# Later steps for softmax sums that go by DRAM, an earlier root in an output loop, and a depthwise stage cut differently

## The chip, the cores and the metric

The kernel runs on one core of one Trainium2 chip. The metric is the device time in microseconds (us), the median of several runs. The profile comes from one further execution. Its engines are PE (matrix products), DVE (vector), ACT (activation functions and copies), POOL and SP, which here only issues transfers (DMA). Each engine works through its own instructions in program order, and waits for others by semaphores.

## The reference, cut to what matters

Four layers follow each other on x of shape (4, 256, 64, 64); every layer is added to its input, and takes the input after a group norm. Two pieces of it are what the change touches most: the softmax of layer 0's attention, and the depthwise and pointwise products of layer 2.

```python
# layer 0, after a 3x3 convolution, group norm and relu (xs)
f = jnp.einsum('bnc,bcm->bnm', theta_x, phi_x)
attn = jax.nn.softmax(f, axis=-1)
y = jnp.einsum('bnm,bmc->bnc', attn, g_x)
...
w_y = group_norm(conv1x1(y, w_w, w_b), gn2_w, gn2_b)
return w_y * 0.1 + xs
# layer 1, the end of it: linear attention, projection, norm over channels
out = jnp.einsum('oc,bchw->bohw', w_out, out) + b_out[None, :, None, None]
out = rmsnorm(out, g_out)
# layer 2: kernels made from the image; dk is (B, C, 3, 3), pk is (B, O, C)
dw = lax.conv_general_dilated(xr, kr, (STRIDE, STRIDE), [(PAD, PAD), (PAD, PAD)], feature_group_count=B * C, dimension_numbers=('NCHW', 'OIHW', 'NCHW'))
out = jnp.einsum('bchw,boc->bohw', dw, pk) + bias[None, :, None, None]
# layer 3: four experts mixed into one 1x1 convolution
```

## The kernel before, in words

An image has 256 channels, two halves of 128 partitions, and 4096 pixels. [...] a matrix product of 512 columns is two passes of PE.

**Images overlap.** While PE works through the attention of image b (`attend`), the rest of image b-1's layers (`tail`) and the convolution of image b+1 (`convolve`, `convolve_second` for image 1) are woven into it. Two Python generators do this: `run` takes one step of a `Chain` of layers and one of the attention in turn, and the order in which they call instructions is the order on every engine. For image 3, the last, there is no attention left to hide its tail; instead, 16 output products of image 2 (`held`, filled in by `w.fill` and ended by `w.settle`) are put between its parts.

**The attention** goes through 8 blocks of 512 queries with 16 steps each. A step computes two tiles of logits (`pf`, line 986), ACT takes exp into `pr` (line 987), PE accumulates `py` (line 1096), DVE adds `pr` to `tot` (line 124, the helper `tt`). At the end of a block, `ended_by_dram` divides `py` by the softmax sums. The sums lie across partitions in 128 x 512 values, so they are turned through DRAM: store to `sum_d` (line 1017), reload transposed into `inv` (line 1020), reduce and reciprocal on DVE (lines 1025 to 1027), store to `rec_d` (line 1028), broadcast back (line 1032), multiply (`yq<-yq,inv`), project (`ps_wy`, line 1040), copy into `wt` (line 1041), statistics and store (lines 1003, 1004). Each bare `yield` in it is one step of the next block's attention, so the yields set the place of each instruction in the order of its engine, and of each transfer in SP's queue. The other transfers on that queue are the convolution's filters (line 478, three buffers, loaded one product ahead), image copies (line 661), and loads of layers. The last block of an image takes another way (`ended`).

**The convolution** makes tiles `v` on DVE from rows of the image (`ra`, `rt`), which PE multiplies by the filters `u` into `ps_conv` (line 584 in image 1's, line 512 in the others').

**The output loop of `linear_attention`** goes through 8 blocks of 512 pixels. `outputs` makes the product `ps_o` (line 1339) and four sums of squares on ACT (line 1341). `root` clamps on DVE (line 1346) and takes the power -1/2 on POOL (line 217). `scaled` multiplies by it: for the last image (`alone`) three quarters on ACT (line 1355) and one on DVE (line 1357). `added` transposes on PE (`ps_zt`, line 1368), adds on DVE and takes statistics (line 1370).

**The depthwise stage of the last image, `shared_out`.** There are 8 parts of 1024 pixels: part 2c+h is pixel block c of channel half h. A part is either made on DVE, 8 taps on top of a centre that ACT makes (`taps`, `centre`), or on PE by products with diagonal matrices (`taps_by_products`, line 1557, two halves of 9 products, copied out by ACT on line 1560). Before the change, DVE makes parts 0, 2, 4, 6 and 7, and PE parts 1, 3 and 5. `point` multiplies the two parts of a pixel block by the pointwise kernel `pk` (`ps_pw`, line 1512), which DVE mixes from eight slices (`mix_kernel`); `pointwise_added` adds to the image on DVE (line 1528) and sums squares on ACT (line 1530). All orders in `shared_out` are written out by hand: `diagonal(n)` issues n of PE's products, `go(i, n)` n taps of DVE.

Of the kernel before, what the change touches and what calls it, by code (L numbers as in the profile page):

```python
# [13 lines left out]
P = 128  # L14
NH = 2
HW = 64
# [77 lines left out]
def conv_preact_fast(ctx: ExitStack, tc: tile.TileContext, guard, x, wc, wtpg, ww, wqkv, wout, w1cat, wd2,  # L94
# [864 lines left out]
    def attend(b):  # L959
# [48 lines left out]
        def ended_by_dram(q, py, tot):  # L1008


            at = b * NQ + q
            inv = wk.tile([P, 512], F32, tag="inv", name="inv")
            nc.vector.scalar_tensor_tensor(inv, tot[:, 0:512], 1.0, tot[:, 512:CH], ALU.mult, ALU.add,
                                           accum_out=guard[:, 0, at:at + 1])
            yt = wk.tile([P, 512], F32, tag="yq", name="yq")
            nc.scalar.copy(yt, py)
            nc.sync.dma_start(out=sum_d[at], in_=inv)
            yield
            yield
            nc.sync.dma_start(out=inv.rearrange("r (p k) -> r p k", k=4), in_=sum_d[at].rearrange("p (r k) -> r p k", k=4))  # L1020
            yield
            yield
            yield
            r = sp.tile([P, 4], F32, name="r_inv", bufs=1)
            nc.vector.tensor_reduce(r, inv.rearrange("r (p k) -> r k p", k=4), AX.X, ALU.add)
            nc.vector.reciprocal(r, r)
            nc.vector.tensor_reduce(guard[:, 1, at:at + 1], r, AX.X, ALU.add)
            nc.sync.dma_start(out=rec_d[at].rearrange("(r k) -> r k", k=4), in_=r)
            xc = residual_block(q) if b == B - 1 else None
            yield  # L1030
            yield
            nc.sync.dma_start(out=inv, in_=rec_d[at].partition_broadcast(P))
            yield
            yield
            tt(yt, yt, inv, ALU.mult)
            yield
            wt = k4("wt").rearrange("p (h n) -> p h n", h=NH)
            for h in range(NH):
                ps = bank("ps_wy")
                nc.tensor.matmul(ps, ww_s[:, bass.ts(h, P)], yt, start=True, stop=True)  # L1040
                nc.scalar.copy(wt[:, h, :], ps)
            if b == B - 1:
                for h in range(NH):
                    residual_stats(q, h, xc)
            yield
            projected(q, wt, xc)
# [166 lines left out]
    def linear_attention(w, b, big, qT, k4, st, sh, sums):  # L1213
# [119 lines left out]
        def outputs(c):  # L1333
            zr = sp.tile([P, 4], F32, name="zr", bufs=3)
            banks = []
            for s in range(2):
                ps = bank("ps_o").rearrange("p (j o) -> p j o", j=2)
                for j in range(2):
                    nc.tensor.matmul(ps[:, j, :], qT[:, bass.ts(4 * c + 2 * s + j, P)], w2, start=True, stop=True)  # L1339
                for j in range(2):  # L1340
                    nc.scalar.activation(junk()[:, 0:NH * P], ps[:, j, :], AF.Square, accum_out=zr[:, 2 * s + j:2 * s + j + 1])  # L1341
                banks.append(ps)
            return zr, banks
# [5 lines left out]
        def scaled(zr, banks):  # L1349
            z = k4("z").rearrange("p (j o) -> p j o", j=4)  # L1350
            if alone:
                for j in range(4):
                    src = banks[j // 2][:, j % 2, :]
                    if j < 3:
                        nc.scalar.activation(z[:, j, :], src, AF.Copy, scale=zr[:, j:j + 1])
                    else:
                        nc.vector.tensor_scalar(z[:, j, :], src, zr[:, j:j + 1], None, ALU.mult)
                return z
            for s in range(2):
                tt(z[:, bass.ts(s, 2), :], banks[s], zr[:, bass.ts(s, 2)].unsqueeze(2).to_broadcast([P, 2, NH * P]), ALU.mult)  # L1360
            return z

        def added(c, z, halves=range(NH)):
            cols = bass.ts(c, 512)
            for h in halves:
                pt = bank("ps_zt")
                for j in range(4):
                    nc.tensor.transpose(pt[:, bass.ts(j, P)], z[:, j, bass.ts(h, P)], ident)
                stt(big[:, h, cols], pt, gains[:, 1, h:h + 1], big[:, h, cols], ALU.mult, ALU.add)
                nc.vector.bn_stats(st[:, h, c, :], big[:, h, cols])  # L1370

        if alone:

            this, last = outputs(0), None
            root(this[0])
            for c in range(NC):
                after = outputs(c + 1) if c + 1 < NC else None
                z = scaled(*this)
                for h in range(NH):
                    if last is not None:  # L1380
                        added(c - 1, last, (h,))
                    if h == 0 and after is not None:
                        root(after[0])
                this, last = after, z
                w.settle()
                if c in (2, 4):
                    w.fill(1)
                yield 1
            added(NC - 1, last)
            w.fill(2)  # L1390
            return st
# [20 lines left out]
    def generated(w, b, big, k4, st, sh, diag):  # L1412
# [117 lines left out]
                    nc.scalar.activation(junk(), big[:, oh, cols], AF.Square, bias=pivot[:, oh:oh + 1],  # L1530
                                         accum_out=sums[:, 1, oh, c:c + 1])

        def taps(i):

            c, h = PARTS[i]
            dst = dw[i].rearrange("p (y x) -> p y x", x=HW)
            for ty, tx in TAPS:
                dx = tx - 1
                x0, x1 = max(0, -dx), min(HW, HW - dx)
                k = h * 9 + 3 * ty + tx  # L1540
                stt(dst[:, :, x0:x1], xp[:, h, c * rows + ty:c * rows + ty + rows, x0 + dx:x1 + dx], dk[:, k:k + 1],
                    dst[:, :, x0:x1], ALU.mult, ALU.add)
                yield 0.62

        def taps_by_products(parts):

            for i in parts:
                c, h = PARTS[i]
                dw[i] = k4("dw")
                for s in range(2):  # L1550
                    ps = bank("ps_dw")
                    dst = ps.rearrange("p (y x) -> p y x", x=HW)
                    for n, (ty, tx) in enumerate([(1, 1)] + TAPS):
                        dx = tx - 1
                        x0, x1 = max(0, -dx), min(HW, HW - dx)
                        y0 = (2 * c + s) * RB + ty
                        nc.tensor.matmul(dst[:, :, x0:x1], diag[:, 3 * ty + tx, :], xp[:, h, y0:y0 + RB, x0 + dx:x1 + dx],  # L1557
                                         start=(n == 0), stop=(n == 8))
                        if n == 8:
                            nc.scalar.copy(dw[i][:, bass.ts(s, 512)], ps)  # L1560
                        yield

# [30 lines left out]
        def shared_out():  # L1593

            slices = [load_wp2(j) for j in range(R // 2)]
            yield from w.pending()
            products = taps_by_products([2 * c + 1 for c in range(N // CH - 1)])
            dw[0] = centre(0)
            for k in range(9):
                nc.scalar.activation(diag[:, k, :], ident, AF.Copy, scale=dk[:, 9 + k:10 + k])  # L1600
            on_vector = {i: taps(i) for i in (0, 2, 4, 6, 7)}

            def go(i, n):
                for _ in range(n):
                    next(on_vector[i])

            def diagonal(n):
                for _ in range(n):
                    next(products)

            def point(c):
                d = [dw[2 * c + h] for h in range(NH)]
                return [(2 * c + s, pointwise_products(s, d)) for s in range(2)]

            dw[2] = centre(2)
            diagonal(24)
            go(0, 8)
            w.settle()
            mix_kernel(slices, range(0, R // 2))
            go(2, 3)  # L1620
            mix_kernel(slices, range(R // 2, R))
            go(2, 5)
            dw[4] = centre(4)
            res = point(0)
            diagonal(12)
            pointwise_added(*res[0])
            go(4, 1)
            pointwise_added(*res[1])
            go(4, 7)
            dw[6], dw[7] = centre(6), centre(7)  # L1630
            res = point(1)
            diagonal(18)
            go(6, 1)
            pointwise_added(*res[0])
            go(6, 2)
            pointwise_added(*res[1])
            go(6, 5)
            go(7, 8)
            res = point(2)
            pointwise_added(*res[0])  # L1640
            res = res[1:] + point(3)
            for r in res:
                pointwise_added(*r)

        if diag is None:
            yield from in_order(range(len(PARTS)))
# [752 lines left out]
```

## Time and profile before

| what | us |
|---|---|
| median of 3 runs (3075.39 to 3075.71) | 3075.55 |
| the profiled execution | 3076.46 |
| its span, from first to last instruction | 3073.7 |
| PE busy | 2980.7 (97%) |
| DVE busy | 2071.8 (67%) |
| ACT busy | 1160.1 (38%) |
| image 0's attention with image 1's convolution | about 200 to 714 |
| last image alone | 2807 to the end |

The span is that of one execution, on the profiler's clock from its first instruction. In the views of the profile a group of instructions is named by its source line, engine, operation, and the tiles that it writes and reads (`v<-ra`). A wait names who ended it; in timelines it stands in square brackets with its length. "SPq" and other names with a q are an engine's sequencer, which waits and issues transfers. A transfer's landing is later than its issue.

### The profile page before, as it was taken

Reading aid. Unit: us, or ns where it says so; the run is one execution under the profiler, and the core shown is the slowest. Engines: PE = TensorE matmul, PEld = TensorE weight load, DVE = VectorE, ACT = ScalarE, POOL = GpSimd, SP = SyncE. Lnnn points to the kernel's source line nnn. Section 1 sums busy time; section 2 is a strip of 40 time slices with the busy share of each in tenths; the row PEclk is TensorE's granted clock in tenths of the full one; section 3 lists DMA queues with packets and bytes.
Section 4 is the critical chain, followed back from the end, with each engine's and each line's share of the span. In section 5 each row is a group of like instructions: output and inputs, shape, how many; then the busy total and the mean of one; then the engine's idle time right before and its main releaser. Section 6 shows DMA issues by size and latency. Waiting matters only on the chain.

```text
span 3073.7 us, 24553 instructions
## 1 busy us (share of the span) xinstructions
PE 2980.7 (97%) x8550; PEld 1475.7 (48%) x8550; DVE 2071.8 (67%) x2836; ACT 1160.1 (38%) x2127; POOL 131.8 (4%) x178
## 2 busy tenths in 40 slices
PE   6899999999999999999999999999999999999998
PEld 3454455445554444444566444444446544444643
DVE  8747667852646995777536797678563669866485
ACT  2334233353555332323364532222336453334621
POOL 0100000000010000000011000000000100000100
PEclk9999999999999999999999999999999999999999
DMA  5235433352212233533410333433440232433021
GB/s 220 79 100 128 70 48 50 42 60 79 69 11 35 38 86 65 110 53 61 126 7 11 52 21 86 137 52 41 103 83 18 18 48 38 31 93 99 8 69 66
DMA packets 532387, 200.55 MB, mean 65 GB/s; under 512 B 470688, under 2 KB 480672, under 8 KB 528032
## 3 DMA queue, kind: packets, MB, share of 16 engines
q1 hardware_dynamic: 528224, 182.12, 29.1%
q0 software_dynamic: 4032, 16.78, 3.0%
q8 instruction: 70, 1.15, 0.2%
q14 instruction: 61, 0.50, 0.1%
HBM read 130.13 MB, written 85.52 MB: 70 GB/s over the span
## 4 chain that ended last, share of the span: by engine, by line
PE 70%; DVE 8%; issue 1%; ACT 1%; POOL 0%; DMA 0%; DVEq 0%; POOLq 0%; ACTq 0%
PE pf L986 21%; PE py L1096 20%; PE ps_qkv L1253 5%; PE ps_conv L512 4%; PE ps_pw L1512 4%; PE ps_ex L1712 3%; PE ps_tp L926 3%; PE ps_o L1339 2%; PE ps_g L931 1%; DVE big L127 1%; PE ps_wy L1040 1%; DVE tot L124 1%; PE ps_ctx L1284 1%; PE ps_ss L1244 1%; PE ps_dw L1557 1%
## 5 line engine op out<-in xcount | busy, mean ns | idle before, releaser
L987 ACT ACTIVATE pr<-pf 128x512 f32<-128x512 f32 x1024 | 602.9, 596 | 1117.4 <-PE pf L986 1070.8
L986 PE MATMUL pf<-tpg 128*128 128x512 f32 x2048 | 969.7, 596 | 0.0
L1096 PE MATMUL py<-pr,tpg 128*128 128x512 f32 x2048 | 963.9, 593 | 2.5 <-ACT pr L987 2.3
L124 DVE TENSOR_TENSOR tot<-tot,pr 128x1024 f32<-128x1024 f32 x448 | 546.2, 1219 | 154.4 <-ACT pr L987 153.2
L1096 PEld LDWEIGHTS py<-pr,tpg 128*128 128x128 f32 x2048 | 389.5, 190 | 496.3 <-issue 477.5
L986 PEld LDWEIGHTS pf<-tpg 128*128 128x128 f32 x2048 | 382.5, 190 | 434.1 <-issue 416.3
L127 DVE SCALAR_TENSOR_TENSOR dw<-xp,dk,dw 128x1008 f32<-128x1008 f32 x208 | 263.0, 1268 | 9.8 <-ACT dw L1504 6.9
L512 PE MATMUL ps_conv<-v,u 128*128 128x512 f32 x384 | 170.9, 593 | 3.6 <-DVE v L124 3.6
L1253 PE MATMUL ps_qkv<-wqkv_s,xg 128*128 128x384 f32 x384 | 129.9, 487 | 0.0
L926 PE MATMUL ps_tp<-big,wtpg_s 128*128 128x512 f32 x256 | 117.4, 602 | 3.0 <-ACT big L684 3.0
L124 DVE TENSOR_TENSOR tpg<-ps_g,bg_s 128x512 f32<-128x512 f32 x32 | 22.1, 692 | 145.0 <-PE ps_g L931 145.0
L512 PEld LDWEIGHTS ps_conv<-v,u 128*128 128x128 f32 x384 | 72.8, 190 | 96.1 <-issue 88.5
L217 POOL TENSOR_TENSOR rstd<-rstd,half 128x2 f32<-128x2 f32 x24 | 17.5, 729 | 2334.4 <-DVE rstd L365 2218.0
L1512 PE MATMUL ps_pw<-dw,pk 128*128 128x512 f32 x224 | 101.3, 592 | 0.0
L1253 PEld LDWEIGHTS ps_qkv<-wqkv_s,xg 128*128 128x128 f32 x384 | 72.2, 190 | 53.6 <-issue 9.6
L1272 DVE TENSOR_REDUCE qs<-qk 128x16 f32<-128x512 f32 x24 | 16.5, 686 | 118.5 <-ACT qk L1266 118.5
L927 ACT ACTIVATE tpg<-ps_tp,btp_s 128x512 f32<-128x512 f32 x64 | 43.8, 686 | 119.0 <-PE ps_tp L926 119.0
L584 PE MATMUL ps_conv<-v,u 128*128 128x256 f32 x288 | 68.4, 392 | 10.0 <-DVE v L124 10.0
L926 PEld LDWEIGHTS ps_tp<-big,wtpg_s 128*128 128x128 f32 x256 | 47.6, 193 | 54.8 <-issue 50.3
L1341 ACT ACTIVATE junk<-ps_o 128x256 f32<-128x256 f32 x128 | 49.1, 384 | 63.5 <-PE ps_o L1339 59.1
L1266 ACT ACTIVATE qk<-ps_qkv,rinv 128x256 f32<-128x256 f32 x96 | 45.6, 475 | 72.1 <-PE ps_qkv L1253 58.7
L124 DVE TENSOR_TENSOR v<-ra 128x1024 f32<-128x1024 f32 x58 | 69.5, 1220 | 0.4
(379 smaller groups left out, 3070.5 us busy)
## 6 DMA issues: line engine op xcount, KB each, us to landing
xp<-in_x_dram SPq DMA_DIRECT2D x16, 1024.0 KB, 7.8
wy_d<-wt SPq DMA_DIRECT2D x32, 512.0 KB, 3.0
wy<-wy_d SPq DMA_DIRECT2D x32, 512.0 KB, 4.1
out_dram<-res SPq DMA_DIRECT2D x64, 256.0 KB, 2.1
xs_d<-big POOLq DMA_DIRECT2D x24, 512.0 KB, 11.9
u<-filters SPq DMA_DIRECT2D x48, 256.0 KB, 2.9
xs<-xs_d SPq DMA_DIRECT2D x24, 512.0 KB, 5.0
u<-rows_d SPq DMA_DIRECT2D x36, 256.0 KB, 3.2
```

The lines of the kernel that those rows point to most:

```text
L124: nc.vector.tensor_tensor(o, a, b, op)
L127: nc.vector.scalar_tensor_tensor(o, a, s, b, op0, op1)
L512: nc.tensor.matmul(ps[oh], u(oh, h), v[:, bass.ts(h, 512)], start=(h == 0), stop=(h == NH - 1))
L584: nc.tensor.matmul(ps[:, bass.ts(oh, IY * IX)], u[i][:, h, bass.ts(oh, P)], v[:, i, bass.ts(h, IY * IX)], start=(h == 0), stop=(h == NH - 1))
L926: nc.tensor.matmul(ps, wtpg_s[:, h, k, :], big[:, h, cols], start=(h == 0), stop=(h == NH - 1))
L986: nc.tensor.matmul(pf, phi[:, bass.ts(2 * m + s, P)], theta[:, bass.ts(q, 512)], start=True, stop=True)
L987: nc.scalar.activation(pr[:, bass.ts(s, 512)], pf, AF.Exp)
L1096: nc.tensor.matmul(py, g[:, bass.ts(2 * m + s, P)], probs[i][:, bass.ts(s, 512)], start=(m == 0 and s == 0), stop=(m == NM - 1 and s == 1))
L1253: nc.tensor.matmul(ps[:, 0:3 * HID], xg[:, h, bass.ts(j, P)], wqkv_s[:, h, :], start=(h == 0), stop=(h == NH - 1))
L1339: nc.tensor.matmul(ps[:, j, :], qT[:, bass.ts(4 * c + 2 * s + j, P)], w2, start=True, stop=True)
L1512: nc.tensor.matmul(ps, pk[:, h * NH * P + oh * P:h * NH * P + (oh + 1) * P], dw[h][:, bass.ts(s, 512)], start=(h == 0), stop=(h == NH - 1))
L1712: nc.tensor.matmul(ps, wm[h][:, bass.ts(oh, P)], big[:, h, bass.ts(c, 512)], start=(h == 0), stop=(h == NH - 1))
```

## The change

It has three parts.

In `ended_by_dram`, the reload of the sums is issued one step earlier, and everything from the reduce on comes later: the reduce by two steps, the broadcast by two, the multiplication, the projection and the store by three.

In the last image's output loop, the root of the next block stands ahead of this block's scaling, where it stood between the two channel halves of the block before.

In the depthwise stage, PE leaves two taps of part 1 to DVE (six taps and the centre are 7 products per half, not 9), and the counts of products between the other steps change with it: 27, 5 and 18 where there were 24, 12 and 18. DVE makes part 7 in two halves of 8 rows, and the pointwise products of the last pixel block are issued as they become possible, between additions and taps.

```diff
             nc.sync.dma_start(out=sum_d[at], in_=inv)
             yield
-            yield
             nc.sync.dma_start(out=inv.rearrange("r (p k) -> r p k", k=4), in_=sum_d[at].rearrange("p (r k) -> r p k", k=4))
-            yield
-            yield
-            yield
+            for _ in range(6):
+                yield
             r = sp.tile([P, 4], F32, name="r_inv", bufs=1)
...
             nc.sync.dma_start(out=inv, in_=rec_d[at].partition_broadcast(P))
-            yield
-            yield
+            for _ in range(3):
+                yield
             tt(yt, yt, inv, ALU.mult)
...
                 after = outputs(c + 1) if c + 1 < NC else None
+                if after is not None:
+                    root(after[0])
                 z = scaled(*this)
-                for h in range(NH):
-                    if last is not None:
-                        added(c - 1, last, (h,))
-                    if h == 0 and after is not None:
-                        root(after[0])
+                if last is not None:
+                    added(c - 1, last)
...
-        def taps(i):
+        def taps(i, some=TAPS, over=slice(0, CH // HW)):
...
-            for i in parts:
+            for i, some in parts:
...
-            products = taps_by_products([2 * c + 1 for c in range(N // CH - 1)])
+            products = taps_by_products([(1, TAPS[:6]), (3, TAPS), (5, TAPS)])
...
-            on_vector = {i: taps(i) for i in (0, 2, 4, 6, 7)}
+            on_vector = {i: taps(i) for i in (0, 2, 4, 6)}
+            on_vector[1] = taps(1, TAPS[6:])
...
-            diagonal(24)
+            diagonal(27)
             go(0, 8)
             w.settle()
             mix_kernel(slices, range(0, R // 2))
             go(2, 3)
             mix_kernel(slices, range(R // 2, R))
+            go(1, 2)
             go(2, 5)
             dw[4] = centre(4)
             res = point(0)
-            diagonal(12)
+            diagonal(5)
...
             go(6, 5)
-            go(7, 8)
+
+            ends = [taps(7, TAPS, slice(s * RB, (s + 1) * RB)) for s in range(2)]
+            for _ in ends[0]:
+                pass
             res = point(2)
+            banks = [[bank("ps_pw") for _ in range(NH)] for _ in range(2)]
+
+            def half(s, h):
+                for oh in range(NH):
+                    nc.tensor.matmul(banks[s][oh], pk[:, h * NH * P + oh * P:h * NH * P + (oh + 1) * P],
+                                     dw[6 + h][:, bass.ts(s, 512)], start=(h == 0), stop=(h == NH - 1))
+
+            half(0, 0)
+            half(0, 1)
+            half(1, 0)
             pointwise_added(*res[0])
-            res = res[1:] + point(3)
-            for r in res:
-                pointwise_added(*r)
+            for _ in ends[1]:
+                pass
+            half(1, 1)
+            pointwise_added(*res[1])
+            for s in range(2):
+                pointwise_added(6 + s, banks[s])
```

## The prediction

> **What bounds the kernel now.** I read the page first, then the chain of waits of TensorE (PE) and of VectorE (DVE), then timelines of the three places that the diff touches.
>
> The page, part 1:
>
> ```profile
> PE 2980.7 (97%) x8550; PEld 1475.7 (48%) x8550; DVE 2071.8 (67%) x2836; ACT 1160.1 (38%) x2127; POOL 131.8 (4%) x178
> ```
>
> PE is busy for 2980.7 of 3073.7 us. So an edit is worth the PE idle time that it removes, plus PE work that it removes where PE is the limit. All idle time together is 93 us.
>
> The waits of PE, and those of DVE (total us, times, longest):
>
> ```profile
> PE ps_conv L584 <- DVE v L124: 10.0, 3, 6.7
> ...
> DVE r_inv L1025 <- DMA inv<-sum_d: 39.6, 6, 11.3
> ...
> DVE yq L124 <- DMA inv<-rec_d: 14.9, 5, 5.2
> ```
>
> All eleven DVE stalls on the softmax sums lie in image 0's attention (240 to 700 us); in images 1 to 3 the reduce starts 0.1 to 30 us after its data have landed. Of 54.5 us of DVE stall only three gaps, 10.0 us, reach PE. The longest, in the timelines of DVE, SP's queue and PE, and in the table by windows (PE, PEld, DVE, ACT, POOL busy, then clock):
>
> ```profile
> 326.01 1.05 DVE L1025 TENSOR_REDUCE r_inv<-inv 128x4 f32<-128x512 f32 x1 [11.30 <-DMA inv<-sum_d]
> ...
> 299.76 0.33 SPq L1017 DMA_DIRECT2D sum_d<-inv  x1
> 300.14 0.93 SPq L478 DMA_DIRECT2D u<-filters  x2
> 301.11 1.13 SPq L661 DMA_DIRECT2D xs_d<-in_x_dram  x2
> 302.34 0.54 SPq L1020 DMA_DIRECT2D inv<-sum_d  x1
> 302.92 29.33 SPq L478 DMA_DIRECT2D u<-filters  x2
> ...
> 328.12 6.69 PE L584 MATMUL ps_conv<-v,u 128*128 128x256 f32 x16 [6.72 <-DVE v L124]
> ...
> 320.00:340.00 20.00, 13.28 (x33) 8.06 (x32) 10.02 (x13) 2.71 (x6) 0.00 (x0) 0.74 0.59 58
> ```
>
> The reload of the sums was issued behind 4 MB of image copy and landed at 325.98; DVE stood at the reduce with the convolution's `v` behind it, and PE ran dry for 6.72 us. Then the 16 matmuls took 6.69 us where the other groups of 16 on this line take 3.6: 3.1 us more at half clock. With what surrounds the two shorter gaps (1.98 us at 486, 1.30 at 602; 2.26 and 1.57 by the spacing of matmuls) the stalls cost 9.9 + 2.3 + 1.6 = **13.8 us** of PE time.
>
> The last image's output loop, DVE and POOL:
>
> ```profile
> 2902.35 0.48 DVE L1357 TENSOR_SCALAR ra<-ps_o,zr 128x256 f32<-128x256 f32 x1 [1.11 <-ACT ra L1355]
> 2902.75 0.74 DVE L127 SCALAR_TENSOR_TENSOR tpg<-ps_zt,gains,tpg 128x512 f32<-128x512 f32 x1
> 2903.53 0.69 DVE L1370 BATCH_NORM_STATS2 st<-tpg 128x6 f32<-128x512 f32 x1
> 2904.14 0.15 DVE L1346 TENSOR_SCALAR zr<-zr 128x4 f32<-128x4 f32 x1
> ...
> 2904.46 1.01 POOL L217 TENSOR_TENSOR zr<-zr,half 128x4 f32<-128x4 f32 x1 [3.45 <-DVE zr L1346]
> 2908.92 1.01 POOL L217 TENSOR_TENSOR zr<-zr,half 128x4 f32<-128x4 f32 x1 [3.45 <-DVE zr L1346]
> ```
>
> One turn is 4.46 us and it is a circle: root on POOL (1.01), three scalings on ACT (1.1), DVE's fourth (0.4), its addition and statistics (1.4), the next root's clamp, 0.3 to POOL. No engine is full.
>
> The depthwise stage, PE and DVE, and the mean of a 512-column DVE operation:
>
> ```profile
> 2970.03 7.13 PE L1512 MATMUL ps_pw<-ra,pk 128*128 128x512 f32 x16 [0.65 <-DVE pk L127]
> ...
> 2992.30 1.27 DVE L127 SCALAR_TENSOR_TENSOR dw<-xp,dk,dw 128x1008 f32<-128x1008 f32 x1 [3.26 <-ACT dw L1504]
> ...
> 3004.84 10.43 DVE L127 SCALAR_TENSOR_TENSOR rt<-xp,dk,rt 128x1008 f32<-128x1008 f32 x8
> ...
> L127 DVE SCALAR_TENSOR_TENSOR pk<-wp,pb,pk 128x512 f32<-128x512 f32 x8 | 6.0, 750 | 0.2
> ```
>
> PE has no gap but 0.65 us from 2949 to 3023; its end comes after the last tap of DVE (3015.2) by 16 matmuls, and the last square on ACT ends at 3024.9.
>
> [...] The reload moves 16384 packets of 16 B and lands 11.2 us after its issue on a quiet queue; the store of the same 256 KB lands in 2.0. [...] the trace shows the 16 B packets only after the copy's 64 KB packets (from 315 us).
>
> **Part A, sums by DRAM.** The reload is issued one step earlier (step 0 of the next block, not 1), the reduce is at step 6 instead of 4, the broadcast at 8 instead of 6, the multiplication at 11 instead of 8, the ps_wy matmuls at 12 and the store at 13, of 16 steps: nothing is added. In block 1 the reload now stands ahead of the filters and the copy on SP's queue: sum_d lands at 301.85, so issue 301.9, landing 11.2 us later at 313, and the reduce is due at about 320. In blocks 2 to 5 the reload keeps its place behind filter loads, and the reduce comes two steps later; a step is 4.1 to 4.7 us (blocks of 65 to 75 us), 8.2 to 9.4 us against stalls of 6.7, 4.8, 7.1 and 9.0. The broadcast gets three steps for two: 4 us against stalls of 2.1 to 5.2. So 13.8 us go, less about 1 for rests: **-12.8** (bounds -8 and -13.8).
>
> What is queued behind: in block 1 the two filter loads and the copy [...] land at about 317 and 329; the first product needs its filters at 320.8, the second (335) needs those behind the copy at 330. Slack 4 and 5 us. The reciprocal store, later on SP, lets filter loads pass it.
>
> Images 1 and 2 pay. At the end of their tail and at the convolution's start the statistics of `wt` (two, 1.2 us) and the multiplication (0.6) move nearer to a DVE chain on which PE waits. At 952 us 0.8 us of idle DVE time covers them, 0.4 is left; at 1246 0.3 (1.2 later, 0.9 of PE work earlier). At 1427 the multiplication leaves the chain (-0.6), but the four ps_wy passes (1.72 us) no longer fill PE's time before the gap; afterwards they fill gaps of 0.51 and 0.65, net about +0.3. Sum 1.0 per image, **+2** (0 to +5 [...]).
>
> **Part B, next root first.** The clamp needs only ACT's four squares, which precede the scalings in ACT's order. Then the circle is open and DVE is the limit: 0.06 + 0.4 + 2 x (0.78 + 0.61) = 3.24 us a turn by start distances, ACT 2.04 + 1.1 = 3.1, PE 2.6. Followed from turn 1: turns 2 to 7 begin at 2901.1, 2904.3, 2909.2, 2912.4, 2916.9 and 2920.1 (two `res` operations of 0.65 and waits of 1.0 and 0.6 for ACT in it); the last statistics end at 2926.1 instead of 2930.6. PE's `ps_ex` pieces at the end need 3.4 us from 2921.5 and stay hidden. If PE gets its bank late in turn 4, it is 0.8 less: **-3.7** (-2.5 to -4.8).
>
> **Part C, depthwise.** Four taps less on PE: 8 passes of 0.425, -3.4. DVE gets two taps of 1.305, +2.6, and its eight last taps as sixteen of half width. That size isn't in the trace: the nearest row (512 columns, 0.750 and a gap of 0.04) gives 0.78 at 504, half the 1008 gives 0.65; I take 0.78, so +2.1. ACT's squares come earlier because part 3 ends after 32 products, not 36: part 6's centre is ready at 2988.3, not 2992.2, and DVE's stall of 3.26 goes. DVE begins part 6 at 2991.6, ends the first half of part 7 at 3010.5, two additions at 3011.7, the second half at 3018.0, the last six additions at 3021.7; the squares on ACT, 0.85 each from 3018.8, end at 3023.9: **-1** (-3.2 with 0.65; +1 if PE's half(1,1) or a copy delays DVE).
>
> **Sum** -12.8 + 2 - 3.7 - 1 = **-15.5**. The profiled execution took 3076.46 (2.8 outside its span), 0.9 above the median; against the median 3075.55 this gives **3060**. A measurement of this kernel can hardly tell less than 0.2%, 6.2 us, from no change.
>
> **Rivals.** (1) The stalls move, not vanish: DVE is busy for 14 to 20 of 20 us in image 0, so it may be DVE's work itself that is late; then A gives 0 to -5 and the time is 3067 to 3073. For it: at 590 to 610 DVE is busy 19.7 of 20. Against: those three gaps all follow a stall. (2) SP's order, slower: [...] the reciprocal store waits for a later reduce, and filter loads behind either come after their product. They land about 3 us after issue and products lie 10 to 14 us apart; it decides once the queue holds a load more than 7 us longer. Ten products in image 0 and in the two other convolutions, each 2 us late, are +20 against -15.5: 3080. Against: SP now waits up to 42.8 us at this store and no PE wait names a filter. (3) C turns into a loss with B small: 3064.
>
> **How the numbers follow.** Forecast (3053 to 3067, case 3 within) 0.75; rival 1 0.17; rival 2 0.05; other 0.03. Of rival 1 about half is within 0.2% (above 3069.4). Faster 0.86, same 0.09, slower 0.05. Range 3053 to 3070: both ends of A and B, and half of rival 1.
>
> **What would show it.** DVE's waits on inv<-sum_d and inv<-rec_d below 5 us in all; no 6.7 us gap and full clock at 320 to 340; POOL roots 3.2 to 3.6 us apart; DVE taps of about 0.78 us; the gap before part 6 gone. Wrong, if PE waits name u<-filters, or gaps before ps_conv stay.

## The result, and the profile after

The changed kernel takes 3058.91 us (median, 3058.19 to 3059.73) against 3075.63 for the kernel before: a ratio of 0.9945, 95% interval 0.9929 to 0.9961, 16.7 us or 0.55% faster. The forecast was 3060, 15.5 faster.

Where the time went is read from places that both programs pass. Each row gives what the profile of after has gained on that of before, in us, up to that place ("the sums" of the depthwise stage are its sums of squares, which the last mean needs):

| place | gained so far | in this stretch |
|---|---|---|
| first attention product of image 0 | 1.45 | 1.45, start-up: no code of the change runs there |
| end of image 0's attention | 15.23 | 13.78 |
| end of image 2's attention | 15.30 | 0.07 (1.42, then -1.35) |
| last image, first output product | 14.37 | -0.93 |
| last image, mean after the output loop | 17.53 | 3.16 |
| first depthwise product | 16.37 | -1.16 |
| end of the depthwise sums | 17.96 | 1.59 |
| last product | 16.67 | -1.29 |

So image 0 gave all of its 13.8, the loop 3.2, the depthwise stage 1.6; and there are two losses that no step of the prediction has, after the loop and after the last mean. Without the start-up the change itself has gained 15.2 at the last product, and 15.0 in a second profile of the same kernel (`after_again`, run 7). The page, part 1:

```profile
PE 2976.0 (97%) x8542; PEld 1474.7 (48%) x8542; DVE 2076.1 (68%) x2846; ACT 1159.3 (38%) x2127; POOL 131.7 (4%) x178
```

PE's busy time fell by 4.7 us only; the rest of the gain is idle time. DVE's list of waits has one line left for the softmax sums, 2.9 us where it had 39.6 and 14.9:

```profile
DVE r_inv L1023 <- DMA inv<-sum_d: 2.9, 1, 2.9
```

and PE's list no longer has the wait for `v` on line 584, 10.0 us before. The block of image 0 with the 6.72 us gap, in the timelines of SP, DVE and PE and the table by windows (PE, PEld, DVE, ACT, POOL busy, then PE's clock, DMA share, GB/s):

```profile
297.97 0.33 SPq L1017 DMA_DIRECT2D sum_d<-inv  x1
300.04 0.37 SPq L1019 DMA_DIRECT2D inv<-sum_d  x1
300.46 9.24 SPq L478 DMA_DIRECT2D u<-filters  x2
...
320.04 1.07 DVE L1023 TENSOR_REDUCE r_inv<-inv 128x4 f32<-128x512 f32 x1
...
319.78 3.62 PE L584 MATMUL ps_conv<-v,u 128*128 128x256 f32 x16
...
320.00:340.00 20.00, 20.00 (x64) 11.79 (x63) 12.83 (x19) 5.97 (x10) 0.00 (x0) 1.00 0.45 130
```

The reload is issued as soon as the sums have landed, and lands itself 11.5 us later (311.55); the reduction starts at 320.04 without a wait, and PE is full at full clock.

The output loop, DVE and PE at its end. A pass is one record of PE; the trace has two for each product (the 24 products that open the depthwise stage before are 48 records).

```profile
2886.64 0.15 DVE L1344 TENSOR_SCALAR zr<-zr 128x4 f32<-128x4 f32 x1
2889.86 0.15 DVE L1344 TENSOR_SCALAR zr<-zr 128x4 f32<-128x4 f32 x1
2894.61 0.16 DVE L1344 TENSOR_SCALAR zr<-zr 128x4 f32<-128x4 f32 x1
2898.33 0.17 DVE L1344 TENSOR_SCALAR zr<-zr 128x4 f32<-128x4 f32 x1 [0.41 <-ACT junk L1339]
...
2913.07 0.16 DVE L124 TENSOR_TENSOR mv<-mv,sh_in 128x2 f32<-128x2 f32 x1
...
2908.18 5.85 PE L1729 MATMUL ps_ex<-big,wmh 128*128 128x512 f32 x8
2913.87 0.28 PE L348 MATMUL pm<-mv,avg 128*128 128x2 f32 x2
```

The roots' clamps come 3.2, 4.8 and 3.7 apart (a turn with a `res` operation is longer) instead of 4.4 to 4.5 each. At the end DVE has the mean's input at 2913.23, but PE takes the mean at 2913.87: eight `ps_ex` passes stand before it and take 5.85 us. They take 3.60 in run 8, at full clock, and took 4.59 in the kernel before.

The depthwise stage's end, DVE and PE, and last the mean in the kernel before:

```profile
2987.62 6.21 DVE L127 SCALAR_TENSOR_TENSOR rt<-xp,dk,rt 128x504 f32<-128x504 f32 x8
...
2994.96 6.21 DVE L127 SCALAR_TENSOR_TENSOR rt<-xp,dk,rt 128x504 f32<-128x504 f32 x8
...
3001.23 1.98 PE L1648 MATMUL ps_pw<-rt,pk 128*128 128x512 f32 x4 [0.39 <-DVE rt L127]
3008.26 0.59 PE L348 MATMUL pm<-mv,avg 128*128 128x2 f32 x2 [5.05 <-DVE mv L124]
...
3026.23 0.38 PE L348 MATMUL pm<-mv,avg 128*128 128x2 f32 x2 [2.99 <-DVE mv L124]
```

Eight taps of half a part take 6.21, 0.78 each. PE is done 5.05 us before the last mean, where it was 2.99 before; the mean's products take 0.59 instead of 0.38, and of the `ps_ex` passes after it six follow each other at 0.85 us or more before the distance falls to 0.43, where three did before.

### The profile page after: what moved, and what is told of

It is laid out like the page before. It is cut to its first block, busy times and chain, and to the rows that moved or that the text cites. A ratio compares the mean times of both kernels' runs of the same rounds, so it can differ in the third digit from the quotient of the medians.

```text
span 3057.4 us, 24563 instructions
## 1 busy us (share of the span) xinstructions
PE 2976.0 (97%) x8542; PEld 1474.7 (48%) x8542; DVE 2076.1 (68%) x2846; ACT 1159.3 (38%) x2127; POOL 131.7 (4%) x178
## 3 DMA queue, kind: packets, MB, share of 16 engines
q8 instruction: 70, 1.15, 0.2%
## 5 line engine op out<-in xcount | busy, mean ns | idle before, releaser
L931 PEld LDWEIGHTS ps_g<-wtpg_s,big 128*128 128x128 f32 x512 | 62.2, 192 | 15.3 <-issue 15.3
```

The lines of the kernel that those rows point to most:

```text
L931: nc.tensor.matmul(ps[:, j, :], big[:, h, bass.ts(4 * c + j, P)], wtpg_s[:, h, 2, :], start=(h == 0), stop=(h == NH - 1))
```

## The experiments

In the diffs, an unchanged line has no sign. The time of the kernel before, beside each group of runs, stands with it.

**1. The sums' steps alone.** The kernel before with that hunk of the change.

> Kernel before with the new steps of the sums by DRAM alone (reload one step earlier, reduction at step 7, product at step 13); output loop and depthwise stage as before. My theory: the whole gain of this part is image 0's, where PE waited 9.9 us in block 1, 2.3 in block 2 and 1.6 in block 3 for VectorE's v, and images 1 to 3 give nothing [...]: 3075.6 - 13.8 = 3061.8, range 3060 to 3064; the wait for v is gone from PE's list and the reduction of block 1 begins within 0.5 us of its turn. Rival (stalls move, later blocks pay or the remainder of the attention slows): 3067 or more.

Measured: 3062.76 (3062.18 to 3067.24) against 3074.68, ratio 0.9963 (0.9949 to 0.9978): 11.9 faster. The forecast time came out; the difference of the medians is 1.9 short of 13.8, and the range reaches 5 us up. In the trace image 0 gives 13.8 (12.76 at the end of its attention, having started 1.02 later), the images 1 to 3 lose 0.8, and the rest up to the last product keeps what there was; after it, this profile took 9.8 us to the end of the span where the one before took 7.4. So 2.4 us in this execution are the program's close, not the part's doing. The rival is out.

**2. The other two parts.** The kernel after with the sums' old steps.

> Kernel after with the old steps of the sums by DRAM: the next root first and the changed depthwise stage alone. My theory: the output loop gives 3.2 and the depthwise stage 1.6, of which up to 2.5 goes back where PE comes out of a longer pause at half clock (ps_h after the output loop, the last ex after the last mean): a net gain of 2 to 5, 3070.6 to 3073.6, and 3072.5 if the two paybacks are as in the kernel after. Together with the run of the sums' steps alone the gains should add to the whole 16.7 within 1.5. Rival (the parts need each other, as the sums' steps leave other work for the output loop): the two gains together miss the whole by more than 2.

Measured: 3070.69 (3068.64 to 3072.05), ratio 0.9986 (0.9979 to 0.9993): 4.0 faster. With run 1 this makes 15.9, so the parts add. The traces agree: counted from the first attention product, run 1 gains 13.17 up to the last product, this kernel 1.87 in the last image, from its first mean (2814.04 before) on, together 15.0, and the whole change 15.2. This profile also shows something else, which is in its time though no part made it: from the end of image 0's attention to that of image 1's it gains 3.1 us, though every instruction there is that of before. The timeline of PE at image 1's mean, in this kernel:

```profile
1431.04 0.38 PE L348 MATMUL pm<-mv,avg 128*128 128x2 f32 x2 [3.04 <-DVE mv L124]
1431.28 1.96 PE L986 MATMUL pf<-tpg 128*128 128x512 f32 x4
1433.08 1.88 PE L1096 MATMUL py<-pr,tpg 128*128 128x512 f32 x4
1434.80 0.28 PE L363 MATMUL pv<-ev,avg 128*128 128x2 f32 x2
```

and in the kernel before:

```profile
1430.31 0.58 PE L348 MATMUL pm<-mv,avg 128*128 128x2 f32 x2 [3.04 <-DVE mv L124]
1430.76 3.76 PE L986 MATMUL pf<-tpg 128*128 128x512 f32 x4
1434.31 3.05 PE L1096 MATMUL py<-pr,tpg 128*128 128x512 f32 x4
1437.20 0.28 PE L363 MATMUL pv<-ev,avg 128*128 128x2 f32 x2
```

The same pause of 3.04 us, once with and once without half clock behind it: 3.76 against 6.89 from mean to variance, 3.1 us. The traces' records of the granted clock show where the two differ. In the profiles of before, after and runs 1 to 7 every stretch at half clock ahead of the program's close is 3.41, 6.83 or 10.24 us long, and within one profile all of them begin on one grid of 3.41 us: divided by a third of 10.24, all their times leave the same remainder, 3.06 in before, 1.14 in after, 3.23 in this one. The stretch before (PE's clock 0.50) and the place here where it is missing (1.00), by windows:

```profile
1429.84:1436.67 6.83, 6.36 (x9) 2.95 (x10) 4.41 (x10) 1.19 (x2) 0.00 (x0) 0.50 0.05 19
...
1430.00:1436.80 6.80, 5.76 (x17) 2.90 (x18) 5.70 (x18) 1.20 (x2) 0.70 (x1) 1.00 0.13 52
```

In before and in runs 3, 5 and 6, which have the same pause, 2.1 to 2.6 us of this pause lay ahead of a line of the grid, and the clock fell there (in before PE stopped at 1427.27, and half clock begins at 1429.84); here it was 2.0, at 1430.00, and the clock stayed. How much idle time it takes in general, no run here settles.

**3. The early reload alone.**

```diff
-            yield
             yield
             nc.sync.dma_start(out=inv..., in_=sum_d[at]...)
-            yield
-            yield
-            yield
+            for _ in range(4):
+                yield
```

> Kernel before, only the reload of the sums moved to the step in which they are stored first left the queue (one step earlier); reduction, broadcast and product stay at their old steps. My theory: in image 0's block 1 the reload was late because SP was held by a filter load queued ahead of it; one step earlier it goes ahead of that load and lands at about 311.5 instead of 326, before the reduction's turn at about 311 to 313, so that PE's 9.9 us gap there goes; the 3.8 us of the blocks 2 and 3 (whose broadcast and product come early) stay in part: 3075.6 - 10 = 3065.6, range 3063 to 3067. Rival (only the later steps count, the reload is slow wherever it starts): 3073 or more. Rival (the reload alone is all of it): 3062.

Measured: 3065.0 (3061.37 to 3067.64), ratio 0.9965 (0.9953 to 0.9978): 9.7 faster, the first theory's number. Its waits of DVE, then of PE:

```profile
DVE r_inv L1023 <- DMA inv<-sum_d: 27.6, 4, 9.1
DVE yq L124 <- DMA inv<-rec_d: 13.8, 5, 4.8
...
PE ps_conv L584 <- DVE v L124: 3.0, 2, 2.0
```

The 6.7 us gap is gone, and in the trace image 0 gains 10.18 of the 13.78. The two shorter gaps are still there (they follow the sums of blocks 3 and 4, counted as block 1 is; the expectation calls them 2 and 3), and DVE still stalls 41 us in all, nearly all of it unseen by PE.

**4. The later steps alone.** The reload stays where it was.

```diff
-            yield
-            yield
-            yield
+            for _ in range(5):
+                yield
             r = sp.tile([P, 4], F32, name="r_inv", bufs=1)
...
             nc.sync.dma_start(out=inv, in_=rec_d[at].partition_broadcast(P))
-            yield
-            yield
+            for _ in range(3):
+                yield
```

> Kernel before, only the later steps: the reload stays where it was (second step), reduction, broadcast and product come at the changed kernel's later steps. My theory: the reload of image 0's block 1 still lands at about 326, while the reduction's turn moves from 312 to about 320, so VectorE still stands still for some 4 to 6 us there, and PE waits behind it for less than the 9.9 us of before or not at all, because the v that it had asked for was done by then: 3075.6 - 10, 3063 to 3068. If VectorE's pause falls behind v in every block, all of 13.8 is gained (3062); if the pause still stands ahead of v, 5 or less (3070 or more) and the earlier reload was the half that mattered.

Measured: 3063.1 (3062.95 to 3066.92), ratio 0.9966 (0.9952 to 0.998): 11.6 faster, as much as both halves together (run 1). DVE, SP and PE in block 1:

```profile
301.58 0.53 SPq L1020 DMA_DIRECT2D inv<-sum_d  x1
302.16 21.12 SPq L478 DMA_DIRECT2D u<-filters  x1
...
325.19 1.07 DVE L1024 TENSOR_REDUCE r_inv<-inv 128x4 f32<-128x512 f32 x1 [4.04 <-DMA inv<-sum_d]
...
320.81 3.62 PE L584 MATMUL ps_conv<-v,u 128*128 128x256 f32 x16
324.26 1.88 PE L986 MATMUL pf<-tpg 128*128 128x512 f32 x4
```

The reload lands as late as in the kernel before (325.17), and DVE does stand still for 4.04 us; but `v` was finished by then, and PE has no gap. The times of runs 1, 3 and 4 scatter over 4 to 6 us each, so the traces decide: image 0 gains 13.78 here, as in run 1 and in the whole change. So the earlier reload adds nothing that PE sees: the later steps would have done. The prediction had used it for block 1.

**5. The next root first, alone.**

```diff
+                if after is not None:
+                    root(after[0])
                 z = scaled(*this)
-                for h in range(NH):
-                    if last is not None:
-                        added(c - 1, last, (h,))
-                    if h == 0 and after is not None:
-                        root(after[0])
+                if last is not None:
+                    added(c - 1, last)
```

> Kernel before with the next root put first in the last image's output loop, nothing else. My theory: the loop ends 3.2 us earlier (its last mean at about 2928.2 of the profile, 3.7 predicted), of which 1.2 goes back at once because [...] more of ps_h runs at half clock; net 2 to 3.2: 3072 to 3073.5 against 3075.3. Rival (POOL's pow was not the bound of a turn, the gain in the changed kernel came from the depthwise stage): the last mean moves by less than 1 and the time stays within 0.5 of before. Rival (no payback): 3.7, 3071.6.

Measured: 3073.28 (3071.68 to 3074.44) against 3076.43, ratio 0.999 (0.9981 to 0.9999): 3.15 faster. The trace: from the mean before the loop to the one after it the gain is 3.63 us, and at the last product it is still 3.61 by the same count. I had expected 3.2 and a payback of 1.2; instead the loop gives nearly the prediction's 3.7, with no payback. Its `ps_ex` passes at the end took 4.68 us and the mean waited for DVE, not for PE:

```profile
2922.72 4.68 PE L1711 MATMUL ps_ex<-big,wmh 128*128 128x512 f32 x8
2927.91 0.35 PE L348 MATMUL pm<-mv,avg 128*128 128x2 f32 x2 [0.51 <-DVE mv L124]
```

**6. The depthwise stage alone.** The kernel before with the changed `taps`, `taps_by_products` and shares.

> Kernel before with the changed depthwise stage alone (two taps of part 1 moved from products to VectorE, part 7 and its products in two pieces). My theory: the last mean's input (the sums' end) comes 1.6 us earlier counted from the first depthwise product, but PE is idle for 5 us instead of 3 before that mean and so comes out at half clock for about 3 more passes: 1.3 goes back, net 0 to 1.6 faster, 3073.7 to 3075.3. Rival (the pieces cost more starts than they hide): 1 to 3 slower. Rival (no payback): a full 1.6 to the end.

Measured: 3074.42 (3072.8 to 3075.42), ratio 0.9994 (0.9985 to 1.0002): 2.0 faster by the medians, not told from no change. In the trace the sums end 1.60 earlier, counted from the first depthwise product; PE's pause ahead of the last mean is 5.05, and 0.85 goes back by the last product.

**7. The last part whole again.** The kernel after without the pieces; the moved taps stay.

```diff
-            ends = [taps(7, TAPS, slice(s * RB, (s + 1) * RB)) for s in range(2)]
-            for _ in ends[0]:
+            for _ in on_vector[7]:
                 pass
             res = point(2)
...
             pointwise_added(*res[0])
-            for _ in ends[1]:
-                pass
-            half(1, 1)
-            pointwise_added(*res[1])
-            for s in range(2):
-                pointwise_added(6 + s, banks[s])
+            res = res[1:] + point(3)
+            for r in res:
+                pointwise_added(*r)
```

> Kernel after with part 7 and its products whole again; the two taps of part 1 stay moved. Compare with the kernel after (3058.9). My theory: the pieces let the products and additions of the first half pass under the second half's taps, so that without them the last mean comes 1 to 2.5 later, and PE's pause before it is filled differently: 3059.5 to 3061.5. Rival (the moved shares carry the gain, the pieces give nothing): 3058.9 within 0.5. Rival (the pieces cost): 3058 or less.

Measured: 3057.91 (3056.95 to 3058.55), ratio 0.9941 (0.9924 to 0.9957). My theory had it slower than the kernel after; it isn't. Counted from the first depthwise product the sums end 0.90 earlier than with the pieces, and the last product comes 2.25 earlier. The pause ahead of the mean is short again, and fewer passes behind it run at half clock (3.50 us for four, 3.78 in after):

```profile
3004.51 1.02 PE L1509 MATMUL ps_pw<-rt,pk 128*128 128x512 f32 x2
3008.52 0.38 PE L348 MATMUL pm<-mv,avg 128*128 128x2 f32 x2 [2.98 <-DVE mv L124]
...
3013.20 3.50 PE L1715 MATMUL ps_ex<-big,wmh 128*128 128x512 f32 x4
```

As the two times were from different groups, both kernels were run again side by side:

> The kernel after once more, beside the same with part 7 whole, so that the two are measured on one chip in the same rounds. All theories: 3058.2 to 3059.7 as before; the fixed point of the comparison.

> The kernel after with part 7 and its products whole, once more. Its first profile has the squares' end 0.9 earlier after the first depthwise product than the kernel after, PE's pause ahead of the last mean 2.98 instead of 5.05 and the stretch from that mean to the last product 1.35 shorter. If that is the pieces' doing: 1 to 2.3 less than the kernel after beside it (3056.5 to 3058). Rival (the difference was that of two batches): within 0.5 of it. Rival (my first theory, the pieces hide work): 1 or more above it.

Measured: after 3059.98 (3059.23 to 3060.57), with part 7 whole 3058.51 (3057.2 to 3058.9); the ranges don't overlap, 1.5 us apart. The pieces cost what they were to save, and more: sixteen half taps at 0.78 are 12.4 us of DVE where eight whole ones at 1.30 are 10.4. The gain of the depthwise stage is all the moved taps': 2.49 in the trace (76.09 us from first product to end of sums before, 73.60 here), less 0.90 for the pieces; the second pair of profiles has 2.48 and again 0.90. What came on top in the first profile is not shown to be the pieces' doing. In the second one of this kernel the pause was the same 2.98, and as many passes ran at half clock as behind the pause of 5.05:

```profile
3007.61 0.59 PE L348 MATMUL pm<-mv,avg 128*128 128x2 f32 x2 [2.98 <-DVE mv L124]
...
3012.51 3.78 PE L1715 MATMUL ps_ex<-big,wmh 128*128 128x512 f32 x4
```

There 1.28 went back after the mean, as in the kernel after.

**8. Extra products in PE's pauses.** The kernel after with products of `ones` by `ident` that nobody reads, placed into a bank ahead of the product that waits.

```diff
+    def warm(ps, n):
+        for _ in range(n):
+            nc.tensor.matmul(ps[:, 0:P], ones, ident, start=True, stop=True)
...
         pm = bank("pm")
+        warm(pm, idle[0])
         nc.tensor.matmul(pm[:, 0:NH], avg, mv[:, :, 0], start=True, stop=True)
```

and likewise ahead of `pv`, of `ps_b1`, `ps_hid` and `ps_log` in the last image, and of each `ps_zt` from column 4 on.

> Kernel after with extra products of ones by the identity (128 columns, some 0.22 us each at full clock, nobody reads them) placed in PE's pauses around the means: 17+3+11 in image 0, 16 in each of images 2 and 3, and in the last image 6+3+3 at its first two means, 2 ahead of each half of the output loop's last four columns, 3+6 before ps_h, 20+3+5+2 at the last mean. My theory: the half clock that follows a pause costs 1.7 + 1.5 + 2.6 + 3.5 + 6 + 4 = about 19 us where it shows (excess of the products' start distances over the usual ones after each pause, in the profile of after), and the extra products keep some half to all of it away: 3041 to 3051, most likely 3047; ps_h's products start 0.43 apart all through. Rival (the half clock has another cause than PE's pauses): the same products run at half clock as before, and the extra ones delay the means: 3059 to 3063.

Measured: 3047.22 (3045.46 to 3047.91), ratio 0.9904 (0.9888 to 0.9921), with 260 more instructions on PE. Groups of its `ps_ex` and `ps_h` passes in the last image's stretch, and one of extra products:

```profile
L1746 PE MATMUL ps_ex<-big,wmh 128*128 128x512 f32 x64 | 29.7, 603 | 0.7 <-ACT rt L1361 0.7
L338 PE MATMUL pm<-ident,ones 128*128 128x128 f32 x150 | 17.6, 275 | 0.0
L1455 PE MATMUL ps_h<-tpg,w1n 128*32 128x512 f32 x32 | 5.4, 604 | 0.0
```

and the same groups of after:

```profile
L1729 PE MATMUL ps_ex<-big,wmh 128*128 128x512 f32 x64 | 38.2, 747 | 0.7 <-ACT rt L1353 0.7
L1443 PE MATMUL ps_h<-tpg,w1n 128*32 128x512 f32 x32 | 8.2, 888 | 0.0
```

These two groups are 11.3 us shorter. The profile as a whole has gained 11.3 on that of after at the last product too, but that is a coincidence: counted by place it is 0.8 in the start-up, 1.6 in image 1, 3.0 in image 2 and 5.9 in the last image, where a part of what the passes save goes into waits. The stretches after the means, by windows: at image 2's and at the last image's last mean in this kernel

```profile
2151.00:2161.00 10.00, 9.49 (x24) 4.13 (x23) 4.95 (x14) 6.49 (x8) 3.34 (x4) 1.00 0.25 24
2999.00:3012.00 13.00, 12.35 (x56) 7.55 (x55) 8.94 (x33) 0.43 (x3) 0.70 (x1) 1.00 0.06 23
```

and in after

```profile
2152.00:2162.00 10.00, 9.55 (x19) 4.57 (x20) 4.72 (x14) 2.08 (x3) 0.70 (x1) 0.68 0.00 0
3008.00:3021.00 13.00, 10.12 (x22) 5.37 (x23) 7.46 (x27) 0.36 (x2) 0.69 (x1) 0.61 0.05 20
```

The clock goes from 0.68 and 0.61 to 1.00. In its records after has seven stretches of half clock ahead of the close, this kernel one, of 3.41 us at 2908.1. So in this kernel the half clock behind the pauses came of PE's own idleness: with work in them six of the seven stretches are gone. Of the 19 us of my estimate some 11 came: ahead of `ps_h` the extra products themselves ran at half clock (0.21 apart instead of 0.11 per pass) and held `ps_b1` up by about 1.3, and the wait behind a filled pause stayed (the last mean still stood 0.59 us for DVE behind 4.63 us of extra products).

**9. Both, and the start.** The kernel of run 8 with part 7 whole; and that one with 20 extra products in the 6.83 us between image 0's second mean and its first row product.

> The kernel with the extra products in PE's pauses (3047.2), and part 7 whole. With no half clock to pay after the longer pause, the pieces cost only the direct 0.9 (16 taps of half a part at 0.78 for 8 whole ones at 1.30 are 2.1 more of VectorE, less some 1.2 of hidden products): 3046.3, range 3045.3 to 3047.2. Rival (the pieces' cost is all half clock): 3047.2 within 0.3. Rival (with the clock kept up the pieces gain): 3048 or more.

> The kernel before this one in the list, and 20 extra products in the pause of 6.83 us between the first image's second mean and its first row product (five passes there start 0.84 apart instead of 0.42, 2.3 us in all). Theory of the pauses: the passes run at full clock from the first on, 2.0 to 2.3 less than without, 3044. Rival (the clock cannot be raised that early, or the extra products hold up the first row product): 0 to 1 more than without.

Measured: 3047.72 (3047.19 to 3048.52) and 3044.09 (3043.39 to 3046.38) against 3076.97; ratios 0.9905 (0.9891 to 0.9919) and 0.9894 (0.9878 to 0.991). The first is a miss, and of my making. With part 7 whole PE pauses for 3 us at the last mean (2.98 in run 7), and the 20 extra products made for a 5 us pause take 4.63:

```profile
2995.54 4.63 PE L338 MATMUL pm<-ident,ones 128*128 128x128 f32 x40
3000.00 0.28 PE L353 MATMUL pm<-mv,avg 128*128 128x2 f32 x2
```

The mean comes 2.62 us after the sums' end, 1.30 in run 8: it waited 1.3 for its own filler, which eats the 0.7 that the sums' end gained. So whether the pieces cost anything once the clock is kept up stays open; a run with fewer products was not made. The second came out as expected, and is the fastest kernel of this study: 15.9 below the kernel after beside it (3059.98), 32.9 below the one before.

## Why the prediction was right, and where it was off

**Part A (-12.8 in image 0, +2 in images 1 and 2).** Image 0: 13.78, its upper bound; the rest of about 1 that I kept back did not occur. The mechanism for block 1 was told with one cause too many: the early reload alone removes that gap (run 3), but the later reduction alone removes it too (run 4), with the reload still late. I had followed the reload and not asked whether, at the reduction's new step, `v` would already be done. Images 1 and 2 came to -0.07 in all against +2, and that they nearly cancel is luck. In all six profiles with the later steps and no extra products (after, runs 1 and 4, and three of run 7) image 1 gains 1.3 to 1.4 and image 2 loses 1.3 to 1.7. Of the two small costs on DVE's chains the first came as forecast, 0.31 lost at the place of 952 for 0.4; the second did not, 0.34 gained at that of 1246 for 0.3 lost (after and run 4, in both images). What I did foresee, that `ps_wy` no longer fills the time ahead of the mean, happened in both: the pause grew from 3.04 to 4.25. But the mean of image 1 gained 1.2 to 1.3 and that of image 2 lost 1.5, where I had 0.3 lost at each:

```profile
1414.42 0.56 PE L348 MATMUL pm<-mv,avg 128*128 128x2 f32 x2 [4.25 <-DVE mv L124]
2152.45 0.56 PE L348 MATMUL pm<-mv,avg 128*128 128x2 f32 x2 [4.25 <-DVE mv L124]
```

Half clock lasts 3.41 us at the first and 6.83 at the second, the other way round from before; why is open. Image 3, for which I had nothing, loses 0.47.

**Part B (-3.7).** DVE's side was right: the clamps of turns 2, 3 and 4 are at 2886.64, 2889.86 and 2894.61 against 2886.7, 2889.9 and 2894.8 (the prediction's turns less the 14.37 gained by then). Turns 5 and 6 come 0.3 and 0.8 later than listed, and so do the last statistics, by 0.8, mostly because DVE waits for ACT 2.2 us in all, for 1.6 in the list. So the 0.8 kept back for a bank of PE in turn 4 was used up for another reason, and the aggregation is 3.75 earlier than before by the same count. Alone the part gives 3.63 (run 5). In the changed kernel it gives 3.16, since the step "PE's `ps_ex` pieces need 3.4 us and stay hidden" failed: they took 5.85 at half clock and held the mean by 0.6. That was not so in every execution: in the second profile of run 7's kernel, with the same loop, they took 4.55, the mean waited for DVE, and the loop gave 3.63. The sign that I named for it, roots 3.2 to 3.6 apart, contradicted my own list of turns, which had 3.2 to 4.9; the list was right.

**Part C (-1).** The net was near, 1.59, and its parts were not. The tap of half a part was priced right (0.78 taken, 0.78 measured), and so was part 6's early start (2975.1, for 2975.2 by the prediction's time less the 16.37 gained by then). But I carried the pieces as part of the change without pricing the stage without them: there they lose 0.90, and the moved taps give 2.49.

**What the sum lacked.** 1.16 after the loop (`ps_h` took 8.24 us, 7.05 before) and 1.29 after the last mean went back as half clock; the first was absent, 0.03, in the second profile of run 7's kernel. The prediction counted half clock once, the 3.1 us behind the gap of 6.72 that would close; it didn't ask what the parts' own gains do to PE's pauses. That the forecast is 1.1 from the result is in part luck, from errors of both signs. From 15.5 to the 16.67 gained at the last product: 1.0 and 2.1 better in A, 0.5 worse in B, 0.6 better in C, 2.45 of half clock and 0.93 between image 2 and the last output loop (0.47 of it in image 3) against it, and 1.45 of start-up that no part made.

Of the rivals, the first (stalls move) is out by runs 1 and 4: PE's gaps went and none came elsewhere. (Its ground, DVE busy for 14 to 20 of 20 us in image 0, was misread too: the windows of the kernel before have 10.0 to 19.7.) The second (filters behind the reload) has its blocked queue, 9.24 us from 300.46 in SP's timeline of after (of the 15561 packets that moved from 301 to 309 us all were under 512 B, as the reload's are), yet no PE wait names a filter. The third (C a loss, B small) did not come, though the pieces are a loss.

## What to carry to other kernels

Find, for a late transfer, who is queued behind the instruction that waits for it: moving the waiter past the work that others need gave 11.6 us here (run 4), and 11.9 with the earlier transfer as well (run 1). When an edit shortens one engine's chain, look at how long PE will pause at the next join, since here a pause of 3 to 5 us cost up to 3 us afterwards; a few products that nobody reads, sized to the pause and not beyond it (4.63 us of them in a pause of 3 held the mean up by 1.3 in run 9), gave back some 12 us, against 16.7 for the whole change. And price each half of an edit against the kernel without it, also when the whole comes out right.

## What the runs showed of the hardware that was not expected

- A pause of 3.04 us in the same code left half clock behind in one kernel and none in another (3.1 us). In both the clock changes on a grid of 3.41 us, and it lay differently to the pause: its line came 2.57 us into it in before, where half clock followed, and 2.0 in run 2. In this kernel a difference of 3 us says nothing about an edit until the clock at the place has been read.
- Half clock came without a pause of 3 us, too. In the 6.2 us before the eight passes that end after's output loop PE has gaps of 0.5 to 1.15 us and is busy for 3.73; the clock is 0.50 from 2905.88 to 2912.71, and six of these passes stand 0.85 us or, at the end, 0.56 from the next (5.85 us in all against 3.60 with extra products).
- After the last product the span went on for 7.4 us in one execution and 9.8 in another of nearly the same program, with the same instructions (9.2 and 9.8 in runs 4 and 1, 7.4 to 7.8 in the other profiles).
